# A transformer block with expert-choice routing on one core: gate logits out of the output projection, expert weights loaded behind the last exchange, and a new order of steps

## Chip, core and metric

The kernel runs on one core of a Trainium2 chip. Its time is the device time of one execution in microseconds (us); several runs are given by their median. The engines are named as in the profile: PE (TensorE), DVE (VectorE), ACT (ScalarE), POOL (GpSimd) and SP (SyncE, which here only issues DMAs). A DMA that SP issues goes through one queue of the core.

## What is computed

```python
h = _ln(x, ln1_g, ln1_b) + (silu(t) @ W_ada.T + b_ada)
qkv = (h @ Wqkv.T).reshape(b, n, 3, H, HD)
q, k = _ln(q per head, qn_g, qn_b), _ln(k per head, kn_g, kn_b)
attn = softmax(q @ k.T / sqrt(HD), axis=-1)
o = (attn @ v).reshape(b, n, H * HD)
x = x + o @ Wout.T
tok = x.reshape(-1, d)
gate = softmax(tok @ Wgate.T, axis=-1)
vals, idx = top_k(gate.T, bs // E)
g = _ln(tok[idx], mlp_g, mlp_b)
y = (gelu(g @ fc1s.T + b1s) @ fc2s.T + b2s) * vals
tok = tok.at[idx].add(y)
```

There are 16 sequences of 256 tokens and 256 channels, 16 heads of 64, 8 experts with 1024 hidden channels; each expert chooses 512 of the 4096 tokens. All data is float32.

## The kernel before

**Attention, one sequence after another.** A sequence is two tiles of 128 tokens. Its stages, each a method that `Plan.step` enters with an engine, a cost and what it needs: normalise the tokens and transpose them on PE (`ph`, L581); multiply with the qkv weights (`pm`, L633); normalise q and k per head; scores (`sc`, L754); row maxima on DVE (`nmax`, L762); exponentials on ACT (`pr`, L775); division on POOL; turning the probabilities. Most are turned in blocks of 32 by DVE (`pb`, L796) and then exchanged between partitions by four DMAs of SP (`prT<-pb`, L523); a few are turned on PE (`pp`, L817). Then probabilities times values (`po`, L836), an eviction (`oT`, L869) and, in the class `Tail`, one pass for each of the two tiles:

- `project` (`pw`, L862): 16 products of 128x256 accumulate the output projection;
- `residual` (`tok`, L869): DVE adds x; three buffers of `tok`;
- `store` (`out<-tok`, L873): SP writes the tile to the output;
- `apply` and `store_norm` (`tn`, L546; `xn_dram<-tn`, L883): the tile normalised for the experts, two buffers of `tn`, written to a scratch tensor from which the experts gather;
- `transposes` (`pg`, L888), `evict` (`tokT`, L894, on ACT), `gate` (`pl`, L899) and `gate_evict` (L905): two transpositions of tok on PE, a copy, and two products with the gate weights `wg` (each runs as two instructions), into the one bank "po" that `L836` also uses, give the eight gate logits of each token.

**Two lists for each expert.** The first half of an expert's 512 tokens is the best 256 of the first 30 tiles, all but the last sequence's; the second half is chosen later out of the rest. The gates of the 30 tiles are transposed (`pgT`, L964), and a search bit by bit finds each expert's bound: `reach` (DVE, L1027) compares all gates with a candidate and counts, `pc` (PE, L1036) adds the counts over partitions, `keep` and `drop` (L1042) make the two next candidates, `cand` (L1051) picks one. There are 31 such steps, one after another. They run while the last sequence's attention still goes on, in between its steps; when this work is over, `fill` (L452), some transpositions of the identity whose results nobody reads, stands between the search's products on PE. Then follow `masks`, `scans`, `totals` (L1080 to L1082), `place` (L1088), `turn_places` (`pplace`, L1097), one-hot rows and `list_matmul` (`pls`, L1178), which give the lists `idx`, with more fills between.

**Experts.** 16 jobs, two for each expert, each with 256 tokens: `load` (L1136, L1138, L1140: fc2 and fc1, 1 MB each, and a bias, all issued by SP; the buffers are those of `oT` and `v` of earlier sequences), `gather`, `transposes` (`px`, L1203), `up` (`ph`, L1222, 16 products that run as two instructions each), `gelu`, `down` (`py`, L1238), `finish`, and `scatter`, which adds to the output by an indirect DMA of POOL.

**What sets the order.** The steps are not scheduled while the kernel is built: `PLACES`, a table with one number for each step, written out in the source, is the order in which all are issued (`Plan.order`). Each engine runs its instructions in that order and waits by semaphores where an input or a buffer isn't ready. The costs at the steps (`at(place, engine, cost, ...)`) and their needs don't act on the chip; only the order of issue does.

Of the kernel before, what the change touches and what calls it, by code (L numbers as in the profile page):

```python
# [18 lines left out]
P = 128  # L19
# [45 lines left out]
def kernel(  # L65
    ctx: ExitStack,
    tc: tile.TileContext,
    x: bass.AP,
    small: bass.AP,
    w_adaT: bass.AP,  # L70
    wqkvT: bass.AP,
    woutT: bass.AP,
    fc1T: bass.AP,
# [73 lines left out]
    def make_others():  # L147
# [283 lines left out]
    if True:  # L431
# [422 lines left out]
        class Tail:  # L854
# [3 lines left out]
            def project(self, a=0, b=HP):  # L858
                if a == 0:
                    self.pw = ps.tile([P, D], F32, tag="mm", bufs=3, name="pw")  # L860
# [730 lines left out]
```

## Time and profile before

| | |
|---|---|
| median of 3 runs | 1065.02 us (1064.32 to 1066.86) |
| profiled execution, its own time | 1065.47 us |
| its span | 1063.7 us |
| mean granted PE clock | 0.991 |
| busy, share of the span: PE, DVE, POOL, ACT | 97%, 76%, 58%, 55% |
| instructions on PE | 5625 |
| HBM read, written | 48.56 MB, 12.58 MB |

Start times in the rows count from the start of the span. A row of the time-ordered view has the start, the duration, the engine and line, the operation, the output tile and its inputs, shapes, a count of like instructions, and in brackets the idle time before it with what ended it. Instructions on PE overlap, so the distance from one row's start to the next row's start, and not the printed duration, is what a group costs. A row of the view by windows has the window, its length, the busy time and count of PE, of PE's weight loads, of DVE, ACT and POOL, the granted PE clock, the DMA share and GB/s. A row of the waits has the time waited in total, the number of times and the longest one.

### The profile page before, as it was taken

What the parts mean: (1) busy time and instruction counts of PE and PEld (TensorE: products, weight loads), DVE (VectorE), ACT (ScalarE), POOL (GpSimd) and SP (SyncE); (2) the same over time, 40 slices, a digit from 0 to 9 for tenths busy, and PEclk for the clock granted to TensorE, in tenths of its full rate; (3) what the DMA queues carried; (4) which work ended last, traced back from release to release, by engine and by line L of the source; (5) the groups of instructions that cost most, each with busy time, mean ns of one, the idle gap of its engine ahead of it and who ended that gap; (6) DMA issues with size and microseconds to landing.
All of it is one profiled execution on the core that took longest, in us unless ns stands there. A gap on an engine that the chain in (4) does not pass through costs nothing. (4 is left out here: it accounts for less than half of the span.)

```text
span 1063.7 us, 18664 instructions
## 1 busy us (share of the span) xinstructions
PE 1031.8 (97%) x5625; PEld 692.7 (65%) x5625; DVE 813.1 (76%) x2274; ACT 585.5 (55%) x1645; POOL 612.3 (58%) x973
## 2 busy tenths in 40 slices
PE   9999999999999999999999999997789999999996
PEld 5555656655565565555656556565578888888885
DVE  5778888888988888888888989887375788654540
ACT  2687766667676756758676676756203432233231
POOL 3687666776867666776677767665202333333332
PEclk9999999999999999999999999999889999999998
DMA  6024566675676656665666666667201655665561
GB/s 219 1 53 110 136 154 156 150 170 135 161 175 153 165 139 162 152 158 147 165 158 161 157 155 164 157 175 206 77 33 39 200 158 166 197 193 159 174 203 20
DMA packets 147571, 154.66 MB, mean 145 GB/s; under 512 B 14608, under 2 KB 140816, under 8 KB 147472
## 3 DMA queue, kind: packets, MB, share of 16 engines
q1 hardware_dynamic: 140096, 143.18, 50.9%
q0 software_dynamic: 6144, 8.39, 4.3%
q10 hardware_dynamic: 1232, 1.90, 0.5%
q8 instruction: 45, 0.74, 0.3%
q14 instruction: 54, 0.44, 0.1%
HBM read 48.56 MB, written 12.58 MB: 57 GB/s over the span
## 5 line engine op out<-in xcount | busy, mean ns | idle before, releaser
L633 PE MATMUL pm<-wq,hT 128*128 128x512 f32 x768 | 355.7, 603 | 1.8 <-DVE qk L670 0.7
L775 ACT ACTIVATE pr<-sc,nmax 128x256 f32<-128x256 f32 x512 | 237.8, 480 | 84.3 <-DVE nmax L762 64.4
L786 POOL TENSOR_SCALAR pr<-pr,sums 128x256 f32<-128x256 f32 x512 | 236.5, 481 | 72.1 <-DVE sums L782 62.5
L633 PEld LDWEIGHTS pm<-wq,hT 128*128 128x128 f32 x768 | 138.7, 191 | 149.3 <-issue 127.3
L101 POOL TENSOR_TENSOR ss<-ss,neghalf 128x8 f32<-128x8 f32 x128 | 210.4, 1644 | 10.6
L762 DVE TENSOR_REDUCE nmax<-sc 128x2 f32<-128x512 f32 x256 | 166.8, 672 | 21.2 <-PE sc L754 20.8
L796 DVE STREAM_TRANSPOSE pb<-pr 128x512 f32<-128x512 f32 x232 | 156.8, 691 | 13.7 <-POOL pr L786 9.6
L836 PE MATMUL po<-prT,v 128*64 128x256 f32 x1024 | 126.7, 389 | 5.2 <-DMA prT<-pb 5.2
L754 PE MATMUL sc<-kT,qT 64*128 64x256 f32 x1024 | 128.5, 390 | 0.0
L1255 POOL DMA_INDIRECT out<-y,idx x32 | 51.3, 1602 | 121.1 <-DVE y L1249 69.9
L754 PEld LDWEIGHTS sc<-kT,qT 64*128 64x128 f32 x1024 | 93.6, 186 | 37.1 <-issue 13.8
L1222 PE MATMUL ph<-xT,w 128*128 128x256 f32 x512 | 117.6, 383 | 0.1
L862 PE MATMUL pw<-wo,oT 128*128 128x256 f32 x512 | 116.1, 382 | 0.3 <-DVE qk L670 0.3
L1238 PE MATMUL py<-w,hid 128*128 128x256 f32 x512 | 116.4, 380 | 0.0
L836 PEld LDWEIGHTS po<-prT,v 128*64 128x64 f32 x1024 | 68.5, 138 | 67.8 <-issue 16.3
L862 PEld LDWEIGHTS pw<-wo,oT 128*128 128x128 f32 x512 | 95.8, 190 | 21.3 <-issue 6.1
L1229 ACT ACTIVATE hid<-ph,few 128x256 f32<-128x256 f32 x128 | 60.4, 474 | 87.5 <-PE ph L1222 82.4
L775 ACT ACTIVATION_READ_ACCUMULATOR pr<-sc,nmax 128x1 f32 x512 | 107.9, 211 | 0.0
L646 ACT ACTIVATE sq<-pm 128x512 f32<-128x512 f32 x128 | 77.2, 605 | 54.8 <-PE pm L633 53.8
L650 DVE TENSOR_REDUCE ss<-sq 128x8 f32<-128x512 f32 x128 | 85.2, 669 | 25.6 <-ACT sq L646 25.3
L1222 PEld LDWEIGHTS ph<-xT,w 128*128 128x128 f32 x512 | 95.3, 190 | 13.1 <-ACT xT L1210 0.4
L1238 PEld LDWEIGHTS py<-w,hid 128*128 128x128 f32 x512 | 95.5, 190 | 12.7
(147 smaller groups left out, 1090.7 us busy)
## 6 DMA issues: line engine op xcount, KB each, us to landing
prT<-pb SPq DMA_DIRECT2D x464, 128.0 KB, 2.7
w<-in_fc2T SPq DMA_DIRECT2D x16, 1024.0 KB, 5.7
w<-in_fc1T SPq DMA_DIRECT2D x16, 1024.0 KB, 8.3
qraw<-kb SPq DMA_DIRECT2D x120, 128.0 KB, 2.7
kT<-kb SPq DMA_DIRECT2D x120, 128.0 KB, 2.7
xs<-in_x SPq DMA_DIRECT2D x16, 256.0 KB, 3.3
out<-tok SPq DMA_DIRECT2D x32, 128.0 KB, 2.5
xn_dram<-tn SPq DMA_DIRECT2D x32, 128.0 KB, 2.5
```

What stands on the lines that cost most here:

```text
L101: nc.gpsimd.tensor_tensor(dst, src, neghalf[:, : src.shape[1]], ALU.pow)
L633: nc.tensor.matmul(self.pm, hTs[self.b][:, c, bass.ts(self.t, P)], wq[:, c, bass.ts(self.g, GW)], start=(c == 0), stop=(c == DC - 1),)
L650: nc.vector.tensor_reduce(self.ss[:, 0, :], self.sq.rearrange("p (q e d) -> p e q d", q=QB, e=8), AX.XY, ALU.add,)
L754: nc.tensor.matmul(self.sc[i, j][:, t, :], qTs[self.b][rows, hp, bass.ts(t, P)], keys[rows, hp] if direct else keys[rows, hp // 4, hp % 4] ...
L762: nc.vector.tensor_reduce(self.nmax[i, j], self.sc[i, j], AX.X, ALU.max, negate=True)
L775: nc.scalar.activation(dst, src, AF.Exp, bias=self.nmax[i, j][:, t : t + 1], scale=1.0, accum_out=self.sums[i][:, 0, j, t : t + 1],)
L786: nc.gpsimd.tensor_scalar(self.pr[i, j][:, t, :], self.pr[i, j][:, t, :], self.sums[i][:, 1, j, t : t + 1], 1.0, ALU.mult, ALU.mult,)
L796: nc.vector.transpose(self.pb[i][:, :, :, j].rearrange("p k c t n -> p t k c n"), self.pr[i, j].rearrange("p t (k c m) -> p t k c m", c=TB ...
L836: nc.tensor.matmul(self.po[j * HD : (j + 1) * HD, i, :], vs[self.b][:, c, bass.ts(4 * self.d + 2 * i + j, HD)], prT[:, j, c] if self.whole ...
L862: nc.tensor.matmul(self.pw, oTs[self.b][:, hp // 2, self.t, hp % 2, :], wo[:, hp, :], start=(hp == 0), stop=(hp == HP - 1),)
L1222: nc.tensor.matmul(self.ph[f], self.w1[:, c, bass.ts(f, P)], self.xT[:, c, :], start=(c == 0), stop=(c == DC - 1),)
L1238: nc.tensor.matmul(self.py[i], self.hid[:, f, bass.ts(i, P)], self.w2[:, f, :], start=(f == 0), stop=(f == FC - 1),)
```

## The change

**Gate logits.** The projected tile is 264 columns wide instead of 256. A new class `Fold`, once at the start, loads the output projection untransposed (`wout`, 1 MB, into a buffer of `oT`), multiplies it by the gate weights in 16 products with eight columns, and DVE puts the result beside the projection weights (`wo[:, :, D:]`). So the eight last columns of `pw` are the attention's part of the logits. The part of x itself is added by two products of transposed x with `wg` (L892) into the same eight columns, after the first of the 16 products; transposed x is a new input, of which SP loads 256 KB for each sequence, 40 us ahead of the projection by the planned places. `gate_evict` copies the eight columns out of `pw`. The transpositions `pg`, the copy `tokT` and the products `pl` are gone, and with them the buffers of tokT.

**Loads and fills.** The cost of the first two jobs' loads in the plan is another, and the fills ahead of each step of the first list and the first job are now needs of that step: a fill is issued before it. The fill ahead of `turn_places` has 20 instead of 12 transpositions. `bw` has one buffer instead of two.

**Order.** `PLACES` is new throughout, so that all engines' steps stand in another order. Line numbers are a little higher: L862 is L886, L869 is L899, L873 is L903, L523 is L541, L1036 is L1047, L1136 is L1147.

```diff
+        class Fold:
+            def load(self):
+                self.w = seq.tile([P, DC, H * HD], F32, tag="oT", bufs=2, name="wout")
+                nc.sync.dma_start(self.w, wout.rearrange("(c p) f -> p c f", p=P))
+            def matmul(self):
+                self.pf = ps.tile([P, HP, E], F32, tag="mm", bufs=3, name="pf")
+                for hp in range(HP):
+                    for c in range(DC):
+                        nc.tensor.matmul(
+                            self.pf[:, hp, :], self.w[:, c, bass.ts(hp, P)], wg[:, c, :],
+                            start=(c == 0), stop=(c == DC - 1),
+                        )
+            def evict(self):
+                nc.vector.tensor_copy(wo[:, :, D:], self.pf)
...
+            def load(self):
+                xTs[self.b] = seq.tile([P, DC, N], F32, tag="xT", bufs=2, name="xT")
+                nc.sync.dma_start(
+                    xTs[self.b],
+                    xT[:, self.b * N : (self.b + 1) * N].rearrange("(c p) n -> p c n", p=P),
+                )
...
+                self.pw = ps.tile([P, D + E], F32, tag="mm", bufs=3, name="pw")
+                for hp in range(HP):
                     nc.tensor.matmul(
                         self.pw, oTs[self.b][:, hp // 2, self.t, hp % 2, :], wo[:, hp, :],
                         start=(hp == 0), stop=(hp == HP - 1),
                     )
+                    if hp == 0:
+                        for c in range(DC):
+                            nc.tensor.matmul(
+                                self.pw[:, D:], xTs[self.b][:, c, bass.ts(self.t, P)],
+                                wg[:, c, :], start=False, stop=False,
+                            )
...
             def gate_evict(self):
-                nc.vector.tensor_copy(gates[:, self.n, :], self.pl)
+                nc.vector.tensor_copy(gates[:, self.n, :], self.pw[:, D:])
...
-            at(ROUTE + 60 + n * 80, "SP", 1.5, jobs[n].load, (), [("w", n)], [("oT", B + n), ("v", B + n)], lag=6.0)
+            at(ROUTE + 60 + n * 80, "SP", 6.2, jobs[n].load, (), [("w", n)], [("oT", B + n), ("v", B + n)], lag=2.5)
...
-        at(top + 1.5, "PE", 1.3, partial(fill, 12), ["totals"], (), [("sc", 98, 40)], lag=0.22)
+        at(top + 1.5, "PE", 2.2, partial(fill, 20), ["totals"], ["f1"], [("sc", 98, 40)], lag=0.22)
...
-        3439, 3438, 3441, 3531, 3443, 3445, 3444, 3447, 3449, 3450, 3442, 3446, 3451, 3505,
```

On SP, before, from the last exchanges of attention to the stores of its last tiles; `w` and `b` are the weights and the bias of the first two jobs, `pb` and `prT` the two sides of an exchange:

```order
L523 DMA prT<-pb 128x1x256 x8
L1136 DMA w_8231<-in_fc2T 128x8x256
L1138 DMA w_8233<-in_fc1T 128x2x1024
L1140 DMA b_8235<-in_b2s 128x256
L523 DMA prT<-pb 128x1x256 x4
L873 DMA out<-tok 128x256
L883 DMA xn_dram<-tn 128x256
L1136 DMA w_8528<-in_fc2T 128x8x256
L1138 DMA w_8530<-in_fc1T 128x2x1024
L1140 DMA b_8532<-in_b2s 128x256
L873 DMA out<-tok 128x256
L883 DMA xn_dram<-tn 128x256
```

After, at the same place:

```order
L541 DMA prT<-pb 128x1x256 x4
L878 DMA xT<-in_xT 128x2x256
L1147 DMA w_8362<-in_fc2T 128x8x256
L1149 DMA w_8364<-in_fc1T 128x2x1024
L1151 DMA b_8366<-in_b2s 128x256
L903 DMA out<-tok 128x256
L913 DMA xn_dram<-tn 128x256 x2
L903 DMA out<-tok 128x256
L913 DMA xn_dram<-tn 128x256
L1147 DMA w_9040<-in_fc2T 128x8x256
L1149 DMA w_9042<-in_fc1T 128x2x1024
L1151 DMA b_9044<-in_b2s 128x256
```

The last exchange stood behind the first of the two loads and now stands ahead of it, with the load of transposed x between them. The load that came first was the second job's (the products below show whose weights are used when); now it is the first job's. Between the two loads stood one output tile and one normalised tile; now there are two outputs and three normalised tiles.

On DVE, before, at the residuals of the last sequence's two tiles (`tok<-pw,xs`) within the search:

```order
L869 TENSOR_TENSOR tok<-pw,xs_6621 128x256
L534 BN_STATS st<-tok 128x6
L536 BN_AGGR mv<-st 128x2
L546 TENSOR_SCALAR tn<-tok,mv,rs 128x256
L1027 TENSOR_SCALAR reach,cnt<-gates_86,cand 128x257
L1042 TENSOR_SCALAR keep<-cand 128x1
L1042 TENSOR_SCALAR drop<-cand 128x1
L869 TENSOR_TENSOR tok<-pw,xs_6621 128x256
L534 BN_STATS st<-tok 128x6
L536 BN_AGGR mv<-st 128x2
L1051 SCALAR_TENSOR_TENSOR cand<-pc,drop,keep 128x1
L1027 TENSOR_SCALAR reach,cnt<-gates_86,cand 128x257
```

After:

```order
L564 TENSOR_SCALAR tn<-tok,mv,rs 128x256
L899 TENSOR_TENSOR tok<-pw,xs_6610 128x256
L552 BN_STATS st<-tok 128x6
L554 BN_AGGR mv<-st 128x2
L1053 TENSOR_SCALAR keep<-cand 128x1
L1053 TENSOR_SCALAR drop<-cand 128x1
L1062 SCALAR_TENSOR_TENSOR cand<-pc,drop,keep 128x1
L1038 TENSOR_SCALAR reach,cnt<-gates_86,cand 128x257
L916 COPY gates<-pw 128x8
L1053 TENSOR_SCALAR keep<-cand 128x1
L1053 TENSOR_SCALAR drop<-cand 128x1
L899 TENSOR_TENSOR tok<-pw,xs_6610 128x256
```

The residuals stand at the same steps of the search, the first one now ahead of `cand` instead of behind it. Where a normalised tile (`tn`) followed the first residual, one now stands ahead of it, and the copies of the gates out of `pw` have come in. Each residual reuses the buffer of a tile three earlier.

On PE, before, between the first job (weights w_8528) and the second (w_8233):

```order
L1203 MATMUL px<-ident,xg 128x128 x4
L1238 MATMUL py<-w_8528,hid 128x256 x8
L452 MATMUL fill<-ident 128x128 x8
L1238 MATMUL py<-w_8528,hid 128x256 x8
L452 MATMUL fill<-ident 128x128 x24
L1222 MATMUL ph<-xT,w_8233 128x256 x10
L1178 LDWEIGHTS oh
```

After (weights w_8362 and w_9042):

```order
L1214 MATMUL px<-ident,xg 128x128 x4
L1249 MATMUL py<-w_8362,hid 128x256 x8
L448 MATMUL fill<-ident 128x128 x6
L1249 MATMUL py<-w_8362,hid 128x256 x8
L1233 MATMUL ph<-xT,w_9042 128x256 x10
L1189 LDWEIGHTS oh
```

The 24 fills between the two jobs are gone, and the eight between the first job's two output tiles are six.

More of the change, by code (lines that the diff above doesn't have):

```diff
@@ L68 @@
     x: bass.AP,
+    xT: bass.AP,
     small: bass.AP,
@@ L72 @@
     woutT: bass.AP,
+    wout: bass.AP,
     fc1T: bass.AP,
@@ L439 @@
         wq = attw.tile([P, DC, 3 * H * HD], F32, name="wq")
-        wo = attw.tile([P, HP, D], F32, name="wo")
-        xs, hTs, qTs, kTs, vs, oTs = {}, {}, {}, {}, {}, {}
+        wo = attw.tile([P, HP, D + E], F32, name="wo")
+        xs, xTs, hTs, qTs, kTs, vs, oTs = {}, {}, {}, {}, {}, {}, {}
         def load_x(b, queue=nc.sync):
@@ L452, in fill @@
                 nc.tensor.transpose(pt[:, bass.ts(i % 4, P)], ident, ident)
+        class Fold:
[12 more added lines that the diff above has]
+                nc.vector.tensor_copy(wo[:, :, D:], self.pf)
+        fold = Fold()
         class Shift:
@@ L497, in last_loads @@
             load_x(2)
-            nc.sync.dma_start(wo, woutT.rearrange("(h p) d -> p h d", p=P))
+            nc.sync.dma_start(wo[:, :, :D], woutT.rearrange("(h p) d -> p h d", p=P))
+            fold.load()
             for b in (3, 4):
@@ L856, in __init__, with project @@
                 self.b, self.t, self.n = b, t, b * TB + t
-            def project(self, a=0, b=HP):
-                if a == 0:
-                    self.pw = ps.tile([P, D], F32, tag="mm", bufs=3, name="pw")
-                for hp in range(a, b):
+            def load(self):
[4 more added lines that the diff above has]
+                )
+            def project(self):
+                self.pw = ps.tile([P, D + E], F32, tag="mm", bufs=3, name="pw")
+                for hp in range(HP):
                     nc.tensor.matmul(
@@ L865, in project @@
                     )
+                    if hp == 0:
[4 more added lines that the diff above has]
+                            )
             def residual(self):
                 self.tok = work.tile([P, D], F32, tag="tok", bufs=3, name="tok")
-                nc.vector.tensor_tensor(self.tok, self.pw, xs[self.b][:, self.t, :], ALU.add)
+                nc.vector.tensor_tensor(self.tok, self.pw[:, :D], xs[self.b][:, self.t, :], ALU.add)
                 self.norm = Norm(self.tok, "l2")
@@ L883, in store_norm @@
                 nc.sync.dma_start(xn_dram[bass.ts(self.n, P), :], self.tn)
-            def transposes(self):
-                self.pg = ps.tile([P, D], F32, tag="mm", bufs=3, name="pg")
-                for c in range(DC):
-                    nc.tensor.transpose(
-                        self.pg[:, bass.ts(c, P)], self.tok[:, bass.ts(c, P)], ident
-                    )
-            def evict(self):
-                self.tokT = work.tile([P, D], F32, tag="tokT", name="tokT")
-                nc.scalar.copy(self.tokT, self.pg)
-            def gate(self):
-                self.pl = ps.tile([P, E], F32, tag="po", name="pl")
-                for c in range(DC):
-                    nc.tensor.matmul(
-                        self.pl, self.tokT[:, bass.ts(c, P)], wg[:, c, :],
-                        start=(c == 0), stop=(c == DC - 1),
-                    )
             def gate_evict(self):
-                nc.vector.tensor_copy(gates[:, self.n, :], self.pl)
+                nc.vector.tensor_copy(gates[:, self.n, :], self.pw[:, D:])
         class Gates:
@@ L1243, in weigh @@
             def weigh(self):
-                self.bw = moe.tile([P, KL, D], F32, tag="bw", name="bw")
+                self.bw = moe.tile([P, KL, D], F32, tag="bw", bufs=1, name="bw")
                 for i in range(KL):
@@ L1263 @@
             mm=3, sc=4, po=1, xs=5, hT=2, qT=2, kT=2, v=2, oT=2, xn=4, sq=2, ss=4, qk=3, nmax=8,
-            sums=4, pr=PRB, pb=3, qraw=2, prT=4, tok=3, tn=2, tokT=2, pa=1, l1=4, l2=4,
+            sums=4, pr=PRB, pb=3, qraw=2, prT=4, tok=3, tn=2, xT=2, pa=1, l1=4, l2=4,
         ))
@@ L1285 @@
         at(-998, "SP", 4.0, last_loads, (), [("wq", 3), ("x", 2), ("x", 3), ("x", 4)])
+        at(-1e3, "LXW", 0.0, nothing, (), ["wout"], [("oT", -1)], lag=23.0)
+        at(35.0, "PE", 1.65, fold.matmul, ["wout"], ["fold"], [("oT", -1), ("mm", -5)], lag=0.22)
+        at(37.0, "DVE", 0.15, fold.evict, ["fold"], ["wog"], [("mm", -5)])
         for g in range(4):
@@ L1378 @@
                 n = (b, t)
-                pw, tok, tn, tokT, l2, pg, pl = ("mm", 4) + n, ("tok",) + n, ("tn",) + n, ("tokT",) + n, ("l2",) + n, ("mm", 5) + n, ("po", 1) + n
-                at(p, "PE", 3.47, a.project, [("oT", b)], [pw], [pw, ("oT", b)], lag=0.22)
+                pw, tok, tn, l2 = ("mm", 4) + n, ("tok",) + n, ("tn",) + n, ("l2",) + n
+                if t == 0:
+                    at(p - 40, "SP", 0.65, a.load, (), [("xT", b)], [("xT", b)], lag=3.0)
+                at(p, "PE", 3.77, a.project, [("oT", b), ("xT", b), "wog"], [pw], [pw, ("oT", b), ("xT", b)], lag=0.22)
                 at(p + 4, "DVE", 1.0, a.residual, [pw], [tok], [pw, ("xs", b), tok, l2], lag=0.15)
@@ L1385 @@
                 at(p + 7, "SP", 0.5, a.store_norm, [tn], [("xnd", b)], [tn], lag=2.0)
-                at(p + 6, "PE", 0.22, a.transposes, [tok], [pg], [tok, pg], lag=0.22)
-                at(p + 7, "ACT", 0.3, a.evict, [pg], [tokT], [pg, tokT], lag=0.19)
-                at(p + 8, "PE", 0.45, a.gate, [tokT], [pl], [tokT, pl], lag=0.22)
-                at(p + 9, "DVE", 0.16, a.gate_evict, [pl], [("gates", b)], [pl])
+                at(p + 4.5, "DVE", 0.16, a.gate_evict, [pw], [("gates", b)], [pw])
         marks.append(len(plan.steps))
@@ L1421 @@
         at(top, "DVE", 1.12, first.masks, [("cand", 0)], ["masks"], [("pb", 99, 0)])
-        at(top + 1, "PE", 0.1, first.totals, ["masks"], ["totals"], [p1], lag=0.22)
+        at(top + 1, "PE", 0.1, first.totals, ["masks", "f0"], ["totals"], [p1], lag=0.22)
         at(top + 2, "DVE", 1.35, first.scans, ["masks"], ["scans"], [("pb", 99, 0)])
         at(top + 3, "DVE", 1.12, first.place, ["totals", "scans"], ["place"], [p1, ("pb", 99, 0)])
-        at(top + 4, "PE", 0.9, first.turn_places, ["place"], ["turnp"], [p2, ("pb", 99, 0)], lag=0.22)
+        at(top + 4, "PE", 0.9, first.turn_places, ["place", "f1"], ["turnp"], [p2, ("pb", 99, 0)], lag=0.22)
         at(top + 5, "DVE", 0.85, first.split, ["turnp"], ["split"], [p2])
-        at(top + 0.5, "PE", 1.3, partial(fill, 12), [("pc", 0)], (), [("sc", 98, 39)], lag=0.22)
-        at(top + 1.5, "PE", 1.3, partial(fill, 12), ["totals"], (), [("sc", 98, 40)], lag=0.22)
-        at(top + 4.5, "PE", 1.6, partial(fill, 16), ["turnp"], (), [("sc", 98, 50)], lag=0.22)
+        at(top + 0.5, "PE", 1.3, partial(fill, 12), [("pc", 0)], ["f0"], [("sc", 98, 39)], lag=0.22)
+        at(top + 1.5, "PE", 2.2, partial(fill, 20), ["totals"], ["f1"], [("sc", 98, 40)], lag=0.22)
+        at(top + 4.5, "PE", 1.6, partial(fill, 16), ["turnp"], ["f2"], [("sc", 98, 50)], lag=0.22)
         at(ROUTE + 90, "DVE", 1.14, first.choose, ["place", ("idx", 0)], ["chosen"], [("pb", 99, 0), ("pb", 99, 1)])
@@ L1445 @@
                 if n == 0:
-                    at(k + 1.5 + i, "PE", 0.44, partial(fill, 4), [("oh", 0, i)], (), [("sc", 98, 80 + i)], lag=0.22)
-                at(k + 1 + i, "PE", 0.14, partial(a.list_matmul, 5 * i, 5 * i + 5), [("oh", n, i), ("give", n)] + ([("pls", n, i - 1)] if i else []), [("pls", n, i)], [pls, oh], lag=0.22)
+                    at(k + 1.5 + i, "PE", 0.44, partial(fill, 4), [("oh", 0, i)], [("f3", i)], [("sc", 98, 80 + i)], lag=0.22)
+                at(k + 1 + i, "PE", 0.14, partial(a.list_matmul, 5 * i, 5 * i + 5), [("oh", n, i), ("give", n)] + ([("pls", n, i - 1)] if i else []) + (([("f3", i)] if i else ["f2"]) if n == 0 else []), [("pls", n, i)], [pls, oh], lag=0.22)
             at(k + 10, "DVE", 0.32, a.take, [("pls", n, 5)], [("idx", n)], [pls])
@@ L1451 @@
                 for m in range(2):
-                    at(k + 11 + m, "PE", 1.95, partial(fill, 18), [("pls", 0, 5)], (), [("sc", 98, 60 + 4 * m)], lag=0.22)
-                at(k + 12.5, "PE", 0.9, partial(fill, 8), [("px", 0)], (), [("sc", 98, 70)], lag=0.22)
-            at(k + 12, "PE", 0.44, a.transposes, [("xg", n)], [("px", n)], [px, ("xs", B + n)], lag=0.22)
+                    at(k + 11 + m, "PE", 1.95, partial(fill, 18), [("pls", 0, 5)], ["f4"], [("sc", 98, 60 + 4 * m)], lag=0.22)
+                at(k + 12.5, "PE", 0.9, partial(fill, 8), [("px", 0)], ["f5"], [("sc", 98, 70)], lag=0.22)
+            at(k + 12, "PE", 0.44, a.transposes, [("xg", n)] + (["f4"] if n == 0 else []), [("px", n)], [px, ("xs", B + n)], lag=0.22)
             at(k + 13, "ACT", 1.14, a.evict, [("px", n)], [("jT", n)], [px, ("hT", B + n), ("qT", B + n), ("pr", B + n)])
@@ L1460 @@
         for f in range(FC):
-            at(k + f, "PE", 0.87, partial(jobs[0].up, f), [("jT", 0), ("w", 0), "gelus"], [("ph", f)], [("sc", 99, f), ("hT", B)], lag=0.22)
+            at(k + f, "PE", 0.87, partial(jobs[0].up, f), [("jT", 0), ("w", 0), "gelus", "f5"], [("ph", f)], [("sc", 99, f), ("hT", B)], lag=0.22)
             at(k + f + 0.5, "ACT", 0.48, partial(jobs[0].gelu, f), [("ph", f)], ["hid"], [("sc", 99, f), ("qT", B)])
@@ L1567 @@
         "x": a["x"].reshape(NTOK, D),
+        "xT": a["x"].reshape(NTOK, D).T,
         "small": np.concatenate([vecs] + [
@@ L1574 @@
         "woutT": a["Wout"].T,
+        "wout": a["Wout"],
         "fc1T": a["fc1s"].transpose(0, 2, 1),
```

473 rows, old and new, of the table PLACES are left out of this document.

## Prediction

> **What bounds the kernel now.** I read the page first, for the engine that is busy.
>
> ```profile
> PE 1031.8 (97%) x5625; PEld 692.7 (65%) x5625; DVE 813.1 (76%) x2274; ACT 585.5 (55%) x1645; POOL 612.3 (58%) x973
> ```
>
> PE is the engine that counts; only work taken off it, or idle time before it, can move the time. Next, the busy time by stage: attention up to the transposed gates (734.0), the search for the gate bounds in two pieces, and the expert jobs.
>
> ```profile
> 0.00:734.00 734.00, 728.89 (x3598) 431.29 (x3598) 624.40 (x1261) 487.57 (x1430) 512.28 (x870) 1.00 0.60 148
> 734.00:756.43 22.43, 17.52 (x124) 11.46 (x123) 13.72 (x71) 13.08 (x40) 12.87 (x28) 0.92 0.43 142
> 756.43:774.30 17.87, 9.74 (x56) 8.34 (x55) 3.74 (x18) 0.37 (x1) 0.81 (x2) 0.81 0.44 147
> ...
> 825.00:1063.00 238.00, 228.72 (x1481) 200.14 (x1479) 136.25 (x738) 73.67 (x151) 78.64 (x64) 0.99 0.57 164
> ```
>
> The first number is the length, the second PE's busy time. Attention has 5.1 us without PE in 734; the two search pieces have 4.9 and 8.1 us in only 40. Both have one cause each in PE's waits:
>
> ```profile
> PE pg L888 <- DVE tok L869: 8.4, 2, 8.1
> PE po L836 <- DMA prT<-pb: 5.2, 2, 4.8
> ```
>
> The **exchange wait** (4.8 us) is in the time-ordered rows of SP, DVE and PE, in that order:
>
> ```profile
> 733.03 0.54 SPq L1136 DMA_DIRECT2D w<-in_fc2T  x1
> 733.67 0.64 SPq L1138 DMA_DIRECT2D w<-in_fc1T  x1
> 734.36 1.60 SPq L1140 DMA_DIRECT2D b<-in_b2s  x1
> 736.05 2.54 SPq L523 DMA_DIRECT2D prT<-pb  x4
> ...
> 733.27 0.70 DVE L796 STREAM_TRANSPOSE pb<-pr 128x512 f32<-128x512 f32 x1
> ...
> 732.21 1.95 PE L836 MATMUL po<-prT,v 128*64 128x256 f32 x16
> 744.18 3.35 PE L836 MATMUL po<-prT,v 128*64 128x256 f32 x16 [4.78 <-DMA prT<-pb]
> ```
>
> DVE has turned the last probabilities at 733.97, but SP is issuing a job's weights until 735.96, and the exchange then shares the DMA with 2 MB that went ahead. Its products begin at 744.18 instead of 739.40, and run in 3.35 instead of 1.95 us.
>
> The **store wait** (8.1 us) is the same at the next load (rows of SP, DVE, PE again):
>
> ```profile
> 763.99 0.38 SPq L1136 DMA_DIRECT2D w<-in_fc2T  x1
> ...
> 765.55 0.68 SPq L873 DMA_DIRECT2D out<-tok  x1
> ...
> 766.81 7.51 SPq L873 DMA_DIRECT2D out<-tok  x3
> ...
> 756.43 0.48 DVE L1027 TENSOR_SCALAR_CACHE_REDUCE reach<-gates,cand 128x257 bf16<-128x257 f32 x1
> ...
> 773.05 0.42 DVE L869 TENSOR_TENSOR tok<-pw,xs 128x256 f32<-128x256 f32 x1 [10.57 <-DMA out<-tok]
> ...
> 774.30 0.48 DVE L1027 TENSOR_SCALAR_CACHE_REDUCE reach<-gates,cand 128x257 bf16<-128x257 f32 x1
> ...
> 760.22 3.70 PE L862 MATMUL pw<-wo,oT 128*128 128x256 f32 x16
> ...
> 774.84 0.16 PE L1036 MATMUL pc<-cnt,twice 128*128 128x1 bf16 x1 [0.56 <-DVE reach L1027]
> ...
> 778.65 0.16 PE L1036 MATMUL pc<-cnt,twice 128*128 128x1 bf16 x1
> ...
> 779.65 0.16 PE L1036 MATMUL pc<-cnt,twice 128*128 128x1 bf16 x1
> ```
>
> The last residual needs one of three tok buffers, whose store was issued at 765.55 behind the next job's weights and has landed by 773.05, 7.5 us on. The search stands behind that residual on DVE. The stop has an echo in the granted clock:
>
> ```profile
> 770.00:775.00 5.00, 0.82 (x4) 0.58 (x5) 1.75 (x8) 0.37 (x1) 0.00 (x0) 0.50 0.69 249
> 775.00:780.00 5.00, 4.79 (x32) 4.31 (x32) 3.49 (x21) 0.00 (x0) 0.00 (x0) 0.72 0.05 18
> ```
>
> **The change, part by part**, against the profiled execution (1065.47 us).
>
> *1. Gate logits, to 734.* The pitches come from the starts of consecutive rows:
>
> ```profile
> 416.19 3.72 PE L862 MATMUL pw<-wo,oT 128*128 128x256 f32 x16
> 419.75 1.88 PE L633 MATMUL pm<-wq,hT 128*128 128x512 f32 x4
> 421.46 0.38 PE L888 MATMUL pg<-ident,tok 128*128 128x128 f32 x2
> 421.68 1.88 PE L633 MATMUL pm<-wq,hT 128*128 128x512 f32 x4
> 423.40 0.51 PE L899 MATMUL pl<-few,tokT 128*128 128x8 f32 x4
> 423.77 0.68 PE L633 MATMUL pm<-wq,hT 128*128 128x512 f32 x1
> ...
> 725.85 0.38 PE L888 MATMUL pg<-ident,tok 128*128 128x128 f32 x2
> ...
> 728.39 1.96 PE L633 MATMUL pm<-wq,hT 128*128 128x512 f32 x4
> ```
>
> A pw of 256 columns takes 3.56/16 = 0.2225 us; a column costs 0.83 ns (a pm of 512 takes 1.71/4 = 0.4275), so eight more cost 6.7 ns. A transposition costs 0.22/2 = 0.11, an eight-column product 0.37/4 = 0.0925. In the 30 tails ahead of 734, 60 transpositions go (-6.6), 480 pw instructions grow (+3.2), and the products with transposed x cost what the gate products did (0). Fold adds 16 products in 32 instructions, by the same row 32 x 0.0925 = +3.0. Sum -0.4.
> [...]
> Furthermore tail 14 stands open: from 725.85 to 728.39 PE spends 2.54 us on transpositions and gate products whose work is 4 x 0.11 + 8 x 0.0925 = 1.18; some 1.3 us are waits on DVE and ACT in a chain that disappears: -1.3. The 16 loads of transposed x, the copy and the other pool are off PE. Together -1.7. Bounds: -5 if the new order also takes all idle time of the stage, +3 if every product waits 0.1 us for its x or Fold for its weights.
>
> *2. Exchange wait.* SP issues the exchange as DVE finishes: 733.97 plus 2.54 of issue; the fourth begins some 0.6 before the end, at 735.9, and the median landing is
>
> ```profile
> prT<-pb SPq DMA_DIRECT2D x464, 128.0 KB, 2.7
> ...
> xs<-in_x SPq DMA_DIRECT2D x16, 256.0 KB, 3.3
> ```
>
> so 738.6 against 739.40. The wait and the slow products go, with 0.2 left for jitter: -(4.78 + 1.40) + 0.2 = -6.0. If PE arrives the 1.7 us earlier and DVE doesn't, a part stays: bounds -6.2 to -3. The weights lose their early start, which nothing pays for: the first job's products come only after the place transpositions of 793.89 (a row of term 5).
>
> *3. Store wait.* The last residual now reuses a buffer whose store is issued ahead of any weights. It could begin as pw ends, 763.92; the next reach follows 1.25 later (773.05 to 774.30), at 765.17: 8.74 after the reach at 756.43. Both pw in between are longer by 0.37 + 16 x 0.0067 = 0.48: 9.7. Against 17.87: -8.1, plus 0.2 for the normalised rows that move in. Bounds -8.6 to -5.
>
> *4. Cold clock.* Three search steps take 778.65 - 774.84 = 3.81 us, where one takes 1.00 afterwards: -0.8.
>
> *5. and 6. Fills.*
>
> ```profile
> 792.54 1.51 PE L452 MATMUL fill<-ident 128*128 128x128 f32 x12
> 793.89 1.25 PE L1097 MATMUL pplace<-ident,both 128*128 128x128 f32 x8
> ...
> 822.28 2.78 PE L452 MATMUL fill<-ident 128*128 128x128 f32 x24
> 824.90 4.48 PE L1222 MATMUL ph<-xT,w 128*128 128x256 f32 x20
> ```
>
> 24 fills take 2.62, 0.109 each. They stand between the first job's last product and the second's first; the changed order has none there, and if that product's inputs are there, this is -2.6, and -0.2 for two fewer of eight before (bounds -2.8 to 0, if the job's tokens or weights are late instead). Ahead of the place transpositions stand 20 instead of 12 fills: +0.9, and the further fills tied ahead of the first job's lists and products add about +0.7: +1.65 (0 if the transpositions wait for DVE anyway, +3.5 if all that are tied come on top).
>
> Sum: -1.7 - 6.0 - 7.9 - 0.8 + 1.65 - 2.8 = -17.5; 1065.47 - 17.5 = 1048.0. The profiled execution lies 0.45 above the median of the runs (1065.02): **1047.5**. The low bounds together give -23.4, the high ones -2.3 with the cold clock gone. The terms don't all fall on one side: the root of the summed squares of their distances is 3.8 down and 7.1 up, and these are their ends, so the forecast's own range is 1044 to 1053.
>
> **Rivals.**
> *A wait that takes the place.* The first job's weights now stand ahead of the stores of the last-but-one sequences, and DVE's residual and normalised rows of the last sequence reuse their buffers. For it: the store of 765.55 needed 7.5 us behind such a load. Against: with issue at 736.5 plus 0.65 and about 3 us of weights, the store is issued near 740.2 and lands near 747.7, while the last sequence's first pw, which ends at 760.22 now, ends near 754.2 with the exchange wait gone: 6.5 us of slack. If the load slips by more than that, each further microsecond shows; half the old stop is +4: 1051.5. [...] Chance 0.12.
> *Attention gives it back.* All steps are in a new order; one that costs 5 us more of PE waits in 734 us (it has 5.1 now, so twice as many) gives 1053. Chance 0.12.
> *Slower: the loads of transposed x.* Sixteen loads of 256 KB pass through SP's queue ahead of exchanges. If each delayed an exchange that PE waits for by its 3.3 us, 53 us come on top: 1100. It outweighs the gain from 17.5/16 = 1.1 us each. Against it: sixteen equal loads of x pass there now, and PE waits for exchanges twice in all, 5.2 us. Chance 0.04.
> *It doesn't do what it says*, with both stops kept: then only terms 1, 5 and 6 remain, -2.8, 1062. The order contradicts this; it is counted with attention's rival.
>
> **How the numbers follow.** The forecast has 0.72. The range 1042.5 to 1054 takes in the forecast's own, the first rival and most of the second, with a little below for an order that saves more than I see; about a tenth is left out on each side. A measurement of this kernel tells 0.3% (3.2 us) from no change: faster 0.95 (the forecast, the first rival, nearly all of the second), same 0.01, slower 0.04.
>
> **What would show it.** Right: no wait on the exchange or on a store over 1 us in PE's and DVE's rows after the transposed gates; a granted clock of 1.00 from there to the lists; transposed gates about 1.7 us earlier; about 10 us between the two reaches around the last residuals; no fills between the first two jobs. Wrong: a DVE wait for out or xn stores in the search, PE idle time in attention well over 5 us, or PE waiting for transposed x.

## The result, and the profile after

The changed kernel took 1048.53 us (median of 4 runs, 1045.56 to 1050.92) beside 1064.67 us for the kernel before (4 runs): a ratio of 0.9847, 95% interval 0.9815 to 0.9879. The forecast was 1047.5. The profiled spans are 1046.4 and 1063.7 us: 17.3 less, where the sum of the terms said 17.5.

The windows of the changed kernel, cut at the transposed gates, at the 13th reach, and a little behind the 15th (759.65) and the last reach (774.69) (length, busy time of PE, PE's weight loads, DVE, ACT, POOL, then granted PE clock, DMA share, GB/s):

```profile
0.00:733.18 733.18, 728.81 (x3570) 429.13 (x3570) 621.61 (x1261) 479.56 (x1401) 512.91 (x872) 1.00 0.61 155
733.18:749.77 16.59, 16.10 (x124) 10.90 (x123) 14.09 (x72) 12.63 (x39) 7.47 (x16) 1.00 0.65 208
749.77:759.97 10.20, 9.97 (x60) 8.61 (x58) 4.31 (x19) 0.00 (x0) 0.28 (x2) 1.00 0.03 10
759.97:775.50 15.53, 13.48 (x108) 10.80 (x109) 12.93 (x81) 0.00 (x0) 6.18 (x13) 1.00 0.45 156
```

The two search pieces have shrunk to 16.6 and 10.2 us and PE is busy in nearly all of them; the clock is full. The first row has hardly changed. PE's longest waits are now these:

```profile
PE fill L448 <- POOL ident masks.py:199: 1.4, 1, 1.4
PE po L854 <- DMA prT<-pb: 1.4, 2, 1.0
PE pm L651 <- ACT v L660: 1.2, 1, 1.2
```

The last exchange, rows of SP, DVE and PE: issued at 733.13, 0.06 us after DVE's transposition ends (732.37 + 0.70), with transposed x and the weights behind it; its products wait 0.37 us.

```profile
733.13 2.50 SPq L541 DMA_DIRECT2D prT<-pb  x4
735.67 0.61 SPq L878 DMA_DIRECT2D xT<-in_xT  x1
736.38 1.49 SPq L1147 DMA_DIRECT2D w<-in_fc2T  x1
...
732.37 0.70 DVE L814 STREAM_TRANSPOSE pb<-pr 128x512 f32<-128x512 f32 x1
...
738.87 1.95 PE L854 MATMUL po<-prT,v 128*64 128x256 f32 x16 [0.37 <-DMA prT<-pb]
```

The last residuals, rows of SP and DVE: the output of tile 27, whose buffer the first of them reuses, is issued at 739.05 behind the first weights, 14 us ahead of need. Both residuals now wait for PE's products and not for a store.

```profile
739.05 1.08 SPq L903 DMA_DIRECT2D out<-tok  x1
...
749.77 0.48 DVE L1038 TENSOR_SCALAR_CACHE_REDUCE reach<-gates,cand 128x257 bf16<-128x257 f32 x1
753.64 0.42 DVE L899 TENSOR_TENSOR tok<-pw,xs 128x256 f32<-128x256 f32 x1 [3.05 <-PE pw L886]
758.41 0.42 DVE L899 TENSOR_TENSOR tok<-pw,xs 128x256 f32<-128x256 f32 x1 [2.52 <-PE pw L886]
759.65 0.48 DVE L1038 TENSOR_SCALAR_CACHE_REDUCE reach<-gates,cand 128x257 bf16<-128x257 f32 x1
```

The fills, and tail 14, on PE: 20 fills end where the place transpositions begin; no fills stand ahead of the second job (807.81); and tail 14 runs straight into the next qkv products.

```profile
776.69 2.38 PE L448 MATMUL fill<-ident 128*128 128x128 f32 x20
778.90 1.06 PE L1108 MATMUL pplace<-ident,both 128*128 128x128 f32 x8
...
804.35 3.62 PE L1249 MATMUL py<-w,hid 128*128 128x256 f32 x16
807.81 4.48 PE L1233 MATMUL ph<-xT,w 128*128 128x256 f32 x20
...
722.65 3.36 PE L886 MATMUL pw<-wo,oT 128*128 128x264 f32 x14
725.85 3.60 PE L651 MATMUL pm<-wq,hT 128*128 128x512 f32 x8
```

(The description above speaks of 16 products in a projection: they are eight products that run as two instructions each, so the 16 are instructions, as the working of the prediction counts them. It also speaks of 31 steps of the search; the source and the traces have 30.)

### The profile page after: what moved, and what is told of

It is laid out like the page before. It is cut to its first block, busy times and chain, and to the rows that moved or that the text cites. A ratio compares the mean times of both kernels' runs of the same rounds, so it can differ in the third digit from the quotient of the medians.

```text
span 1046.4 us, 18639 instructions
## 1 busy us (share of the span) xinstructions
PE 1028.9 (98%) x5601; PEld 688.8 (66%) x5601; DVE 810.8 (77%) x2275; ACT 575.9 (55%) x1613; POOL 612.1 (58%) x973
## 5 line engine op out<-in xcount | busy, mean ns | idle before, releaser
L651 PE MATMUL pm<-wq,hT 128*128 128x512 f32 x768 | 350.7, 602 | 1.3 <-ACT v L660 1.2
L814 DVE STREAM_TRANSPOSE pb<-pr 128x512 f32<-128x512 f32 x232 | 157.0, 691 | 11.2 <-POOL pr L804 7.2
L886 PE MATMUL pw<-wo,oT 128*128 128x264 f32 x512 | 127.0, 393 | 0.1
L886 PEld LDWEIGHTS pw<-wo,oT 128*128 128x128 f32 x512 | 93.8, 190 | 23.0 <-issue 6.4
```

Source lines behind the costliest of these rows:

```text
L651: nc.tensor.matmul(self.pm, hTs[self.b][:, c, bass.ts(self.t, P)], wq[:, c, bass.ts(self.g, GW)], start=(c == 0), stop=(c == DC - 1),)
L814: nc.vector.transpose(self.pb[i][:, :, :, j].rearrange("p k c t n -> p t k c n"), self.pr[i, j].rearrange("p t (k c m) -> p t k c m", c=TB ...
L886: nc.tensor.matmul(self.pw, oTs[self.b][:, hp // 2, self.t, hp % 2, :], wo[:, hp, :], start=(hp == 0), stop=(hp == HP - 1),)
```

## The experiments

Twelve kernels, each timed beside the kernel before. In the edits, `row` is the order that PLACES gives, `behind(k, j)` puts step k right behind step j, and `back` is the last exchange. The table has the starts of the transposed gates, of the 5th, 13th, 15th and last reach, of the first job's first product, and the span, all in us:

| kernel | gates | 5th | 13th | 15th | last | first job | span |
|---|---|---|---|---|---|---|---|
| before | 734.09 | 747.93 | 756.43 | 774.30 | 790.11 | 807.02 | 1063.7 |
| b_exchange | 733.79 | 741.77 | 751.67 | 769.39 | 785.58 | 802.48 | 1059.1 |
| b_store | 734.05 | 745.18 | 753.67 | 762.44 | 777.48 | 794.38 | 1051.0 |
| b_both | 734.40 | 742.07 | 752.30 | 761.07 | 776.10 | 793.44 | 1050.0 |
| b_all | 734.40 | 742.06 | 750.84 | 759.61 | 774.65 | 791.58 | 1046.6 |
| b_nogate | 725.34 | 735.85 | 744.35 | 762.15 | 777.95 | 794.87 | 1051.4 |
| a_nogate | 715.38 | 723.60 | 732.36 | 741.13 | 756.13 | 774.26 | 1027.9 |
| after | 733.18 | 741.22 | 749.77 | 759.65 | 774.69 | 792.82 | 1046.4 |
| a_ahead | 734.10 | 749.67 | 758.90 | 768.78 | 783.82 | 801.93 | 1055.6 |
| a_gap | 733.05 | 741.11 | 749.66 | 759.53 | 774.57 | 792.70 | 1049.1 |
| a_onex | 733.98 | 741.64 | 750.42 | 760.30 | 775.33 | 793.50 | 1047.3 |
| a_few | 732.88 | 740.98 | 749.53 | 759.40 | 774.44 | 791.50 | 1045.1 |
| a_split | 733.41 | 741.56 | 750.10 | 752.40 | 769.56 | 788.56 | 1042.2 |
| a_best | 734.44 | 742.55 | 751.11 | 753.40 | 770.57 | 788.82 | 1043.6 |

**The exchange alone (b_exchange).**

```diff
+        behind(step_of(jobs[1].load)[0], back)
```

> The kernel before with one step moved: the load that was issued first (the second job's weights) stands behind the last exchange instead of ahead of it; nothing else differs. Theory (the stall is the exchange queued behind the load): the 4.8 us wait of the products on the exchange goes, with 1.4 us of slow products; the transposed gates stay at 734.1, the 13th reach moves from 756.4 to about 750.4, the store wait of 8 us stays, span about 1057.7 (-6). Rival (a wait takes its place, for instance PE then waits for DVE's turned probabilities or the store wait grows by what is won): less than 2 us gained. If the load was harmless and the exchange late for DVE's sake, nothing changes.

1060.8 us, ratio 0.9961 (0.9948 to 0.9973); span 1059.1, 4.6 less. From the transposed gates to the 5th reach 7.98 instead of 13.84 us: the 5.9 us were there. But from there to the 13th it takes 9.90 instead of 8.50, on PE because of this:

```profile
739.43 1.95 PE L836 MATMUL po<-prT,v 128*64 128x256 f32 x16 [0.32 <-DMA prT<-pb]
...
742.88 1.00 PE L817 MATMUL pp<-ident,pr 128*128 128x128 f32 x4 [0.90 <-POOL pr L786]
```

With the exchange on time PE reaches the next transpositions before POOL has divided their probabilities: the stall had covered a second one. Theory for the stall, a small part of the rival for the rest.

**The store alone (b_store).** `tok14` is the store of tile 28.

```diff
+        behind(step_of(jobs[0].load)[0], tok14)
```

> The kernel before with one other step moved: the load that was issued second (the first job's weights) stands behind the store of the output tile whose buffer the last residual reuses; nothing else differs. Theory (the last residual waits for a store queued behind the weights): DVE's 10.6 us wait and PE's 8.1 us go, with 0.8 us of steps at the low clock: 17.9 us between the 13th and the 15th reach become about 9, span about 1054.8 (-8.9). The exchange wait of 4.8 us stays. Rival (the store wait hides another one, such as the first job's weights coming late for its first products): the reaches come closer, but the first job's products begin less than 4 us earlier.

1053.66 us, ratio 0.9906 (0.988 to 0.9932); span 1051.0. The two reaches are 8.77 us apart (worked out beforehand: 8.74), and the 15 steps behind them take 15.04 instead of 15.81: 9.1 + 0.8. The other 2.7 us lie ahead of the 5th reach, where the edit moved nothing: the exchange wait was 3.46 us in this execution, where the kernel before had 4.78, and the products after it ran at full clock (1.95 us). Each kernel has one trace, and between these two the size of one and the same wait differs by 1.3 us.

```profile
742.83 1.95 PE L836 MATMUL po<-prT,v 128*64 128x256 f32 x16 [3.46 <-DMA prT<-pb]
```

**Both loads (b_both).**

```diff
+        behind(step_of(jobs[1].load)[0], back)
+        behind(step_of(jobs[0].load)[0], tok14)
```

> The kernel before with both loads moved, the one behind the last exchange, the other behind the store. Theory (two independent stalls): the two gains add, -6 and -8.9, span about 1049; what is left to the changed kernel's 1046.4 is the gate logits (about -1) and the fills (about -1.2). Rival (one stall covers part of the other): the sum is smaller by 2 us or more, span above 1051.

1051.06 us, ratio 0.9873 (0.9849 to 0.9898); span 1050.0, 13.7 less. It lies between theory (1049) and rival (1051). What is missing is again ahead of the 13th reach (10.23 us from the 5th): PE waits 1.3 us for POOL, whose rows show five operations on the gates (casts of L944, subtractions of L947) ahead of the divisions; the first, the last and the divisions:

```profile
739.00 0.83 POOL L944 CAST vals<-gate_of 128x224 bf16<-128x224 f32 x1
...
742.36 0.82 POOL L944 CAST vals<-left 128x224 bf16<-128x224 f32 x1
742.96 4.56 POOL L786 TENSOR_SCALAR pr<-pr,sums 128x256 f32<-128x256 f32 x10
```

**Both loads, the casts and the fills, with the old gate logits (b_all).** `parts_` is the step of those casts, `turn` attention's last products on PE.

```diff
+        behind(parts_, turn)
+        for k in row[end:]:
+            if getattr(plan.steps[k][3], "func", None) is fill:
+                run_of(k, nothing)
```

> The kernel before with both loads moved as in the run with both, and two edits more: POOL's split of the gates of the first 28 tiles into three bf16 parts (its casts) stands behind attention's last products instead of ahead of attention's last divisions, and the 24 fills between the first two jobs are left out. The gate logits are still transposed and multiplied as before. Theory (the run with both lost 1.3 us where PE waits for POOL's divisions, which queue behind those casts; the fills cost 2.6): span about 1050.0 - 1.3 - 2.6 = 1046, the changed kernel's 1046.4 to 1 us, although no gate logit is computed the new way: the new gate logits are then worth about nothing in sum. Rival (the new gate logits or the rest of the new order bring what is missing): 1048.5 or more.

1047.39 us, ratio 0.9843 (0.9818 to 0.9868); span 1046.6. The wait for POOL is gone (8.78 us from the 5th to the 13th reach; all eight transpositions run as one row):

```profile
741.56 1.07 PE L817 MATMUL pp<-ident,pr 128*128 128x128 f32 x8
```

Four edits of whole steps in the old kernel, three moved and one kind left out, with its transpositions of tok and its gate products, give what the change gives (0.9847), as far as intervals of 0.005 and 0.006 can tell. So the eight columns, transposed x, Fold and the rest of the new order are together worth about nothing; what each of them is worth by itself is not shown. The sums agree, the stages don't: by the table, the changed kernel has the gates 1.2 us earlier, needs 1.1 us more from the 13th to the 15th reach and 1.2 us more from the last reach to the first job. Behind the second job's first product the kernel of this run loses 1.2 us again; there PE waits 0.93 us for ACT, a wait that neither the kernel before nor the changed one has.

**Without gate work, before and after (b_nogate, a_nogate).**

```diff
+        for k in named("Tail", "transposes") + named("Tail", "evict") + named("Tail", "gate"):
+            run_of(k, nothing)
```

> The kernel before without its gate work: the transpositions, the copy to tokT and the gate products are left out, and eight channels of tok are copied as logits in their place, so the lists are of other tokens; the amount of later work is the same. Theory (PE bounds attention, so its work there counts fully): 30 tails of 0.22 + 0.37 us go ahead of the transposed gates, and 1.3 us of waits in tail 14: the transposed gates at about 715 instead of 734.1, span about 1043 (-19 to -21). Rival (attention waits on other engines, DVE above all, and PE's gate work filled gaps): less than half of it, transposed gates later than 725.

1053.05 us, ratio 0.9893 (0.9868 to 0.9917). The transposed gates come 8.8 us earlier, not 19: the rival, though only just (725.34, where it said later than 725). Of the missing 10 us, 6.1 are idle time of PE ahead of the gates (11.2 us instead of 5.1), which its waits put to DVE and ACT:

```profile
PE pm L633 <- DVE qk L670: 2.9, 6, 1.1
PE sc L754 <- ACT kT L729: 2.5, 1, 2.5
PE ph L581 <- DVE xn L572: 1.1, 2, 1.0
```

Behind the wait of 2.5 us the clock is at half for 3.4 us (721.2 to 724.6), which by my estimate, half of that time, costs another 1.7; the rest was not traced. Exchanges take only 0.6 us there.

```diff
-                self.pw = ps.tile([P, D + E], F32, tag="mm", bufs=3, name="pw")
+                self.pw = ps.tile([P, D], F32, tag="mm", bufs=3, name="pw")
...
+        for k in step_of(fold.matmul) + step_of(fold.evict):
+            run_of(k, nothing)
```

> The changed kernel without its gate work: the eight more columns, the products with transposed x and Fold's products are left out (the loads of transposed x and of the weights for Fold stay), and eight channels of the projection are copied as logits, so the lists are of other tokens. Theory (the new way costs 3.2 us for columns, 11.1 for the products with transposed x and 3.0 for Fold ahead of the transposed gates, all on PE): they come at about 715.9 instead of 733.2, span about 1028 (-18). Then the whole price of the gates is the same before and after to about 1 us. Rival (the small products hide in weight loads or the new way is cheaper than the pitches say): -8 us or less. Rival (PE no longer bounds attention): less than -8 as well, but with waits on DVE or ACT in PE's rows.

1028.8 us, ratio 0.9656 (0.963 to 0.9682); span 1027.9, transposed gates at 715.38: 17.8 us earlier, where 17.3 were expected. In the new order most of the work is on PE's path. That the numbers match so closely is luck: this execution had its first qkv products done 2.2 us later than the changed kernel's (the transpositions behind them begin at 19.54 and 17.32), and counted from there the gate work costs 20.0 us; columns and Fold are dearer than I had worked out (see below). So the price of the gate work can't be read off the pair, as I had meant to: the orders bear its absence differently.

**The load ahead again (a_ahead).**

```diff
+        row.remove(k)
+        row.insert(row.index(back), k)
```

> The changed kernel with one step moved back: the first job's weights are loaded ahead of the last exchange again. Theory: the exchange wait comes back, PE waits 3 to 5 us for the exchange where it waits 0.4 now, and the products run slower after it: span about 1052 (+5 to +6). Rival (the gain of this stage came from the new order of the other engines, not from the load's place): within 2 us of 1046.4.

1057.7 us, ratio 0.9928 (0.9903 to 0.9954); span 1055.6, 9.2 more (0.9 of them ahead of the transposed gates, where nothing was moved): the sign and place of the theory, but dearer. The wait is 6.16 us, and the clock is at half from 744.0 to 750.8, for 6.8 us where the kernel before had 3.4:

```profile
745.58 3.68 PE L854 MATMUL po<-prT,v 128*64 128x256 f32 x16 [6.16 <-DMA prT<-pb]
```

**The fills between the jobs again (a_gap).**

```diff
+        run_of(k, lambda f=plan.steps[k][3]: (f(), fill(24)))
```

> The changed kernel with 24 fills behind the first job's last product, as the kernel before has them. Theory (inputs of the second job's first products are ready, so the fills cost their 0.109 us each): second job's first product 2.6 us later, span about 1049 (+2.6). Rival (the second job's tokens come late and the fills stood in a wait): within 1 us.

1051.44 us, ratio 0.9878 (0.9862 to 0.9895); span 1049.1, 2.7 more. On PE the second job begins 2.62 us after the fills do:

```profile
807.69 2.78 PE L448 MATMUL fill<-ident 128*128 128x128 f32 x24
810.31 4.48 PE L1233 MATMUL ph<-xT,w 128*128 128x256 f32 x20
```

**One load of transposed x (a_onex).**

```diff
+                if self.b:
+                    xTs[self.b] = xTs[0]
+                    return
```

> The changed kernel with transposed x loaded for the first sequence only, so that 15 loads of 256 KB are left out and the logits of other sequences have a wrong part of x; the products stay. Theory (the loads pass through SP's queue beside other work): within 1 us of 1046.4, transposed gates at 733 as before. Rival (each load delays exchanges that PE waits for): up to 15 x 3.3 us faster; by the smaller bound of 0.6 us of issue each, 9 us faster.

1049.72 us, ratio 0.9857 (0.9839 to 0.9876); span 1047.3, transposed gates at 733.98. Nothing is gained: 15 loads of 256 KB were hidden. The slower rival falls.

**Fewer fills, the projections in pieces, and both (a_few, a_split, a_best).**

```diff
+        for i in range(2, 6):
+            run_of(plan.makers["f3", i][0], nothing)
+        run_of(plan.makers["f1"][0], partial(fill, 12))
```

> The changed kernel with fewer fills: 12 instead of 20 transpositions ahead of the place transpositions, and none of the four fills of four between the later list products. Theory (fills that are tied ahead of a step delay it): the place transpositions 0.4 to 0.9 us earlier, the first list about 1.1 us more, first products of the first job 1.5 us earlier, span about 1045 (-1.5). Rival (they hold the granted clock, or stand in time that DVE sets anyway): no change or up to 1 us slower, with the granted clock under 1.00 around the lists.

1048.04 us, ratio 0.9845 (0.982 to 0.9871). In the trace the first job's products stand 1.0 us closer to the last reach (17.06 instead of 18.13); in the median nothing can be told from the changed kernel.

```diff
+        cut = (0, 1, 3, 5, 7, 8)
...
+                run_of(j, partial(a.project, cut[i], cut[i + 1]))
```

> The changed kernel with the last sequence's two projections cut into five pieces each, which stand in the places of the fills of ten search steps, the residuals behind them; nothing is left out. Theory (search steps are a chain through DVE and PE of 1.0 us in which PE has 0.9 us free, so the projections, which hold up two steps by 3.9 us each now, are hidden): the 9.9 us between the 13th and the 15th reach become about 2, ten steps take about 10 us and two residuals of 1 us, span about 1041 (-5 to -6). Rival (pieces delay each step, since the search's product must queue behind a piece on PE): steps of 1.3 us, -2 to -3.

1045.13 us, ratio 0.9811 (0.9784 to 0.9838); span 1042.2. Between 13th and 15th reach there are 2.30 us, and from the 13th to the last 19.46 instead of 24.92: 5.5 gained. A piece fits a step, as these rows of PE show (752.95 to 753.98); a residual costs its step about 1 us (the wait of 0.97):

```profile
752.95 0.16 PE L1049 MATMUL pc<-cnt,twice 128*128 128x1 bf16 x1
752.97 1.14 PE L888 MATMUL pw<-wo,oT 128*128 128x264 f32 x4
753.98 0.16 PE L1049 MATMUL pc<-cnt,twice 128*128 128x1 bf16 x1
...
757.01 0.16 PE L1049 MATMUL pc<-cnt,twice 128*128 128x1 bf16 x1 [0.97 <-DVE reach L1040]
...
787.01 0.55 PE L1216 MATMUL px<-ident,xg 128*128 128x128 f32 x3 [0.99 <-DMA xg<-xn_dram,idx]
```

The last row is what was given back: the gathered tokens came 1 us late, so the span gains 4.2. Why they did wasn't settled.

> The changed kernel with both edits that gained by themselves: the last sequence's projections in pieces between the search steps, and the fewer fills around the first list; nothing is left out. Theory (the two stand in different stages, so they add): -4.2 and -1.3, span about 1041, median about 1043. Rival (with less filling ahead of it, the first job's tokens are what is late, as the 1.0 us wait for gathered tokens in the run with pieces hints): the fills' share is lost, span 1042 or more.

1045.54 us, ratio 0.9819 (0.9803 to 0.9835); span 1043.6. The rival's sign, for other reasons: of the 1.4 us by which the span lies above that of the pieces alone, 1.0 is there at the transposed gates already, where nothing differs; and 18 fills took 3.6 us to the next row, where the next 18 took 2.0, at a low clock (0.82, 0.50 and 0.82 in the three windows of 2 us from 780 on):

```profile
781.01 3.83 PE L448 MATMUL fill<-ident 128*128 128x128 f32 x18
784.64 0.31 PE L1191 MATMUL pls<-give,oh 128*128 128x10 bf16 x5
```

A wait of 0.91 us stands 2.6 us ahead of the fall, but the run with fewer fills alone has the same wait (0.97) and keeps the full clock (1.00 in each window of 2 us from 782 to 794), so the cause isn't shown.

The projections in pieces alone have the lowest median of the kernels that leave no gate work out, 3.4 us under the changed kernel's; the two intervals overlap (0.9784 to 0.9838, 0.9815 to 0.9879), while the traces agree on the stage.

## Why the prediction was right, step by step

Measured against forecast, from the table and the row at 807.81 (before: 824.90): to the transposed gates -0.9 (forecast -1.7); to the 13th reach -5.75 (-6.0); to the 15th -8.0 (-7.9); to the last reach -0.8 (-0.8); to the first job +1.2 (+1.65); to the second job -2.9 (-2.8). The sum was right because most terms were; the first one came near by luck.

*Gate logits.* The mis-sized term, and luck that its sum was near. What it did is smaller still than it looks: five executions of the old order have the gates at 733.79 to 734.40, six of the new one with its loads in at 732.88 to 734.44, so the means differ by 0.6. Two costs were worked out too low. The columns: a projection between the same neighbours, before and after,

```profile
602.36 3.62 PE L862 MATMUL pw<-wo,oT 128*128 128x256 f32 x16
605.82 1.88 PE L633 MATMUL pm<-wq,hT 128*128 128x512 f32 x4
...
601.13 0.61 PE L886 MATMUL pw<-wo,oT 128*128 128x264 f32 x2
601.58 0.51 PE L892 MATMUL pw<-few,xT 128*128 128x8 f32 x4
601.94 3.36 PE L886 MATMUL pw<-wo,oT 128*128 128x264 f32 x14
605.14 1.88 PE L651 MATMUL pm<-wq,hT 128*128 128x512 f32 x4
```

takes 3.46 us before and 0.45 + 3.20 = 3.65 after, the products with x aside: 0.19 more, 5.7 in 30 tails instead of 3.2. (The working took a column's price from products of 512 columns; 0.19/16/8 is 1.5 ns, not 0.83.) And Fold, forecast at 3.0 with a product each 0.0925 us, took 4.51, which is 0.141 for each, and the four products behind it took 3.55 instead of 1.71 (last section): from the first scores that stand ahead of it to the next products with the values the changed kernel takes 16.63 us, the one without gate work 11.82, so 4.8 in sum. With these two prices the term would be about +2.6 instead of -1.7; -0.6 was measured, so some 3 us came back from elsewhere. (Tail 14's waits did go, and are counted.) The start gives 1.7 of them: the transpositions behind the first qkv products begin at 17.9 us on average in the six executions and at 19.6 in the five. That the change is the cause isn't shown, as a_nogate has the new order too and begins them at 19.54. The remainder is open. And the premise that work taken off PE counts in full did not hold for the old order (b_nogate): had the change only taken gate work away there, about half would have been lost, most of it to waits on DVE and ACT. It was not tested by anything I forecast, since the sum of work was near zero.

*Exchange wait.* Right in cause and place (b_exchange, a_ahead). Its size is that of one execution: the same wait was 3.46 us in b_store and 2.83 in b_nogate, and in both the products behind it took 1.95 us, not 3.35. The step that said nothing pays for it was incomplete: about 1.4 us of it reach the end only because the new order also moves POOL's casts behind the divisions. I named no cover that would be gone; b_exchange and b_both show it, b_all that the casts are its cause.

*Store wait, cold clock.* Right to 0.1 us each, and b_store gives them alone.

*Fills.* The 24 fills were pure cost in the changed kernel (a_gap), as forecast; in the old one 0.93 of their 2.6 us comes back as a wait for ACT (b_all). The 20 fills delay the place transpositions (778.90 - 776.61 = 2.3 after the totals, 1.4 before), but the totals follow the last reach 0.4 sooner, so the term is 1.2 where 1.65 was forecast.

*Rivals.* No wait on a store took the old one's place: the store behind the first weights is issued at 739.05 and needed at 753.64. Attention did not give anything back in sum. The loads of transposed x are hidden (a_onex). The exact share of the rest of the new order stays open: b_all leaves within 1 us for it and the gates together, and by the prices above the gates would be the loss in it.

*The range.* The working has a slip: 1047.5 with 3.8 down and 7.1 up is 1043.7 to 1054.6, not 1044 to 1053. Nothing hangs on it, since 1048.53 lies in both.

## What to carry to other kernels

The two large loads cost nothing that shows here once the small transfers stood ahead of them (no wait that the changed kernel's trace lists is for their weights); behind them, one exchange and one store cost 13.7 us (b_both). So look for the small transfer (an exchange, a store that frees a buffer) that is queued next and for who waits on it. A stall that is removed can uncover another, here twice (1.3 us for POOL, 0.9 for ACT): when costing it, list the engine that delivers the step after. And when a change has several parts, put the cheap ones into the old kernel: here four such edits give the whole gain, and the part that took most of the writing adds, with all else that is new in the order, none that can be measured. Where a forecast of small terms comes true, still compare each price with its rows: two were too low here, and the sum did not show it.

## What the hardware showed that I had not expected

In the traces here the granted clock falls to half for stretches of one length or a small multiple of it: the 22 such stretches that windows of the fourteen traces show last 3.4, 6.8 or 10.2 us. For 20 of them that holds to about 0.1 us, by windows of 2 us or less; the two others (b_exchange, b_both) lie in windows of 66 us, from 734 to 800, whose clocks of 0.92 and 0.97 fit 10.2 and 3.4. A further stretch is cut off by the end of the span and not counted: it begins at 1057.7 before and at 1040.1 after. From half-microsecond windows of the run with both loads moved, the first and last with a low clock:

```profile
728.00:728.50 0.50, 0.50 (x2) 0.19 (x1) 0.50 (x1) 0.50 (x1) 0.00 (x0) 0.70 0.77 180
...
731.50:732.00 0.50, 0.50 (x6) 0.43 (x4) 0.23 (x1) 0.00 (x0) 0.00 (x0) 0.89 0.84 215
```

0.70 is 0.30 us at half clock, 0.89 another 0.11, with 3.0 between: 3.4 us. In a_ahead the low clock begins within the stop of 6.16 us, 1.6 us ahead of its end, and lasts two such lengths (0.02 + 6.5 + 0.31 = 6.8). What starts a stretch isn't shown: the waits of tail 14 in the old order, at most 0.6 us each, were followed by one in three executions (b_store, b_both, b_all) and not in two (before, b_exchange).

In the changed kernel such a stretch begins within a run of products of eight columns too, 2.6 us behind its start, though PE has no gap there. Fold, and the windows in which the low clock begins and ends:

```profile
37.36 4.65 PE L463 MATMUL pf<-few,wout 128*128 128x8 f32 x32
41.87 3.76 PE L651 MATMUL pm<-wq,hT 128*128 128x512 f32 x4
45.42 1.06 PE L835 MATMUL pp<-ident,pr 128*128 128x128 f32 x4
...
39.50:40.00 0.50, 0.50 (x7) 0.50 (x6) 0.50 (x3) 0.43 (x2) 0.50 (x1) 0.97 0.00 0
...
46.50:47.00 0.50, 0.50 (x5) 0.50 (x5) 0.50 (x1) 0.48 (x1) 0.00 (x0) 0.71 0.00 0
```

PE is busy throughout, yet runs at half clock for 0.03 + 6.5 + 0.29 = 6.8 us, two lengths again. Fold takes 4.51 us, where 3.0 was forecast and a_few took 3.59 at the full clock, and the four products behind it 3.55 instead of 1.71. All seven kernels here that run Fold have this stretch (one of them, a_few, for one length only), and none of the seven that don't. In a_nogate, without Fold, a wait of 1.50 us for POOL stands there instead, so Fold's whole price is not the sum of these but 4.8. Its products spread among the qkv products would show what of it can be had back; this was not tried.
